# Layer 0 of a two-layer graph attention kernel: units of two heads by half of the rows, with part of the row sums on GpSimd

## The chip, the cores and the metric

The kernel runs on one NeuronCore of a Trainium2 chip. The metric is the device time of one launch in microseconds; lower is better. A core has five engines that run side by side and meet through semaphores: TensorE (PE; its weight loads are shown apart as PEld), VectorE (DVE), ScalarE (ACT), GpSimd (POOL) and SyncE (SP), which here issues most of the DMAs. Each engine works through its own queue in order, so an instruction that waits holds up what is behind it. The working memory SBUF has 128 partitions; PSUM, where TensorE writes its results, has eight banks of 512 f32 per partition.

## The reference

Two attention layers over a graph of N = 2048 nodes, 8 batches, D = 256 features. All values are f32. Shortened:

```python
# layer 0: 8 heads of 32 features; beta = softplus(beta_tilde), adj doubles as the prior
e    = leaky_relu(e_src[:, None] + e_dst[None, :], 0.2) + beta * log(adj + 1e-6)
attn = softmax(where(adj > 0, e, -inf), axis=-1)
h    = attn @ (x @ W[head])                     # per head, then joined
x1   = layernorm(x + h @ W_out.T)
# layer 1: one head
e    = leaky_relu((x1 @ W1) @ (x1 @ W2).T, 0.2)
out  = layernorm(x1 + relu(softmax(where(adj > 0, e, -1e12)) @ (x1 @ W3)))
```

## The kernel before, in words

**Layer 0.** The exponential of a leaky ReLU of a sum is the larger of two products. After common factors are divided out, a weight of head h, key j and query i is `max(c[i], r[j]) * m[j, i] * e[j]`, where c belongs to the query, r and e to the key (both lie in the tile `re`), and m is the masked prior, the same for all heads and batches. The keys lie on the partitions, so 2048 keys are 16 key tiles `jt`, and the queries ("rows" of the attention matrix) lie along the free dimension.

A batch has four head pairs `hp` of two heads. A *step* (`Gat.step`, L355) is one head pair and one key tile. In it VectorE makes `s = max(c, r) * m` for each of the two heads over all 2048 rows (L391), one 128x2048 tile per head; `c` is a row of 2048 numbers copied to all partitions by a DMA (`query_rows`, L325), and `mt` is the transposed prior of this key tile, made once by `make_m` and `make_mt` in batch 0 and read again from DRAM by `load_mt` (L206) for every head pair of every batch. TensorE multiplies s by the values (`products`, L421): `val` collects s times v, where v has been multiplied by e beforehand (`scale`, L303), and `den` collects the row sums, s times e. Each of these matmuls is 32 columns of weights wide and 512 rows long; four of them, two heads by two stretches of rows, stand beside each other on the four 32-partition strips of the array.

For the row sums there is a second way. For the key tiles listed in `SUMMED` (L68), VectorE adds `s * e` into a tile `d` per head (L404; the first of them is written by ScalarE, L409), and TensorE sums `d` once at the end, with weights of one. `SUMMED` is empty for the first head pair of each batch and for batch 0; it has six key tiles in the other head pairs of batch 1 and eight of batches 2 to 7.

When a head pair is done, `finish` (L428) copies val and den out of PSUM on ScalarE, sends den through SBUF and DRAM to be inverted and spread over partitions, and VectorE multiplies. It is a generator; each later step advances it by one stage.

**Layer 1.** The class `Dot` works on the batch before, one query tile of 128 rows per `Dot.step` (L575): TensorE makes scores `e` in four chunks of 512 (L564), between them transposes the last tile's exponentials (`pt`, L590), ScalarE evicts both (`p`, L566, and `pts`, L592), VectorE masks and finds the maximum (L569), ScalarE takes the exponential (L572), and TensorE multiplies by the values into `acc` (L607), which ScalarE evicts into `z` (L612). Between two batches come `output` (layer 0's last product y, L493, and its normalization) and `turn` (the transposes and products that layer 1 starts from).

**The order.** TensorE's order is that of the program text throughout, and from the end of batch 0 on SP's is too (L93, L693). The loop at the end interleaves the layers: it gives each part of layer 1 a number of layer-0 steps to issue after its `acc` (the list at L735, together 64 steps per batch). The order on VectorE, ScalarE and GpSimd is set by the compiler's scheduler, which goes by what is ready and by the order of the text. Batch 0 of layer 0 runs alone, beside the projections of the other batches.

**Buffers.** s tiles come from a ring of eight tiles of 8 KB per partition (tag "s"), which also holds layer 1's p and for some time a tile of heads (`ht`). `mt` has two buffers, c two, and "d" two, which in places also serve as further mt buffers. PSUM: val and den two banks each, acc one, and three banks that all other products share in turn (`mm_tile`, L80).

Of the kernel before, what the change touches and what calls it, by code (L numbers as in the profile page):

```python
# [27 lines left out]
def kernel(  # L28
# [39 lines left out]
    SUMMED = [[()] * NP, [()] + [(0, 3, 6, 8, 11, 14)] * (NP - 1)]  # L68
    SUMMED += [[()] + [tuple(range(0, NT, 2))] * (NP - 1)] * (B - 2)

# [12 lines left out]
    def ring_tile(name, shape=(P, N)):  # L83


        return wide.tile(list(shape), F32, tag="s", name=name, bufs=8)
# [75 lines left out]
    mt_d = dram.tile([N, N], F32, name="mt_d")  # L162
# [4 lines left out]
    rec_d = dram.tile([B, NP // 2, 2, 2, HP, HALF], F32, name="rec_d")  # L167
# [16 lines left out]
    def make_m(jt):  # L184

        a = wide.tile([P, NT, P], I32, tag="d", name="adj_t", bufs=2)
        nc.sync.dma_start(a, adj[:, ts(jt, P)].rearrange("(t p) j -> p t j", p=P))
        m = ring_tile("m", (P, NT, P))
        nc.vector.tensor_scalar(m, a, 0.0, None, ALU.max)
        nc.scalar.activation(m, m, AF.Ln, bias=eps_prior)  # L190
        nc.scalar.activation(m, m, AF.Exp, scale=beta_c)
        nc.vector.scalar_tensor_tensor(m, a, 0.0, m, ALU.is_gt, ALU.mult)
        return m

    def make_mt(jt, m):

        mt = wide_tile("mt", "mt", 2)
        for g in range(NB):
            t = mm_tile("mtp")
            for k in range(IG):  # L200
                nc.tensor.transpose(t[:, ts(k, P)], m[:, g * IG + k, :], ident)
            nc.scalar.copy(mt[:, ts(g, BK)], t)
        nc.sync.dma_start(mt_d[ts(jt, P), :], mt)
        return mt

    def load_mt(jt, tag="mt"):  # L206
        mt = wide_tile("mt", tag, 2)
        nc.sync.dma_start(mt, mt_d[ts(jt, P), :])
# [40 lines left out]
    class Gat:  # L249


        def __init__(self, b):
            self.b = b
            self.units = ((hp, jt) for hp in range(NP) for jt in range(NT))
# [48 lines left out]
        def scale(self, hp):  # L303

            v = self.v[hp].rearrange("p t (a f) -> p t a f", a=HP)
            e = self.re[:, 1, :, ts(hp, HP)]
            nc.vector.tensor_tensor(v, v, e.unsqueeze(3).to_broadcast([P, NT, HP, DH]), ALU.mult)
# [17 lines left out]
        def query_rows(self, h):  # L325

            c = wide_tile("c", "c", 2)
            nc.sync.dma_start(c, c_d[self.b, h:h + 1, :].to_broadcast([P, N]))
            return c

        def load_ahead(self):

            self.mt_loads = (load_mt(jt, "d" if hp == 0 and jt in (4, 5, 8, 9) else "mt")
                             for b in range(self.b, B) for hp in range(NP) for jt in range(NT))
            self.c_loads = (gats[b].query_rows(h) for b in range(self.b, B) for h in range(H))
            self.mts, self.cs_ahead = [], []
            for _ in range(HP):
                self.cs_ahead.append(next(self.c_loads))  # L340
                self.mts.append(next(self.mt_loads))

        def follow(self, gat):

            self.mt_loads, self.c_loads, self.mts, self.cs_ahead = gat.mt_loads, gat.c_loads, gat.mts, gat.cs_ahead
# [9 lines left out]
        def step(self, count=1):  # L355

            for _ in range(count):
                evict()
                hp, jt = next(self.units)
# [3 lines left out]
                if hp == NP - 1 and jt == 0 and self.b + 1 < B:  # L363
# [3 lines left out]
                if at < B * NP:  # L367
                    gat = gats[at // NP]
                    if jt == 4 and gat.b > 0:
                        gat.load(at % NP)  # L370
                    elif jt == 12:
                        gat.scale(at % NP)
                if jt == 0:
                    if self.b > 0:
                        self.cs = [self.cs_ahead.pop(0) for _ in range(HP)]
                    else:
                        self.cs = [self.query_rows(hp * HP + a) for a in range(HP)]
                    self.val = pacc.tile([P, HALF], F32, tag="val", name="val")
# [389 lines left out]
```

## Time and profile before

| what | value |
|---|---|
| median of 3 runs | 4270.26 us (4266.07 to 4271.94) |
| span of the profiled execution | 4267.8 us; the median of the runs is 2.5 us above it |
| TensorE busy | 4169.3 us (98%) |
| VectorE busy | 3617.9 us (85%) |
| ScalarE busy | 1606.5 us (38%) |
| GpSimd busy | 10.3 us (0%) |
| DMA | 843.52 MB, 198 GB/s on average |
| s, L391 | 1024 operations, mean 2341 ns |
| additions to d, L404 | 282 operations, mean 2342 ns |
| val and den matmuls, L424 | 8192 and 5600 records, and 336 for the sums of d |

The profile is one execution of the program. Busy time is the union of an engine's instructions; matmuls overlap in their pipeline and their ends are modelled, so a busy TensorE is not at its peak rate. A matmul of f32 is recorded as two instructions, a transpose as one. Idle time of an engine is put down to what released it last. The span falls into three parts: batch 0 of layer 0 up to about 545 us, seven stretches of 494 us in which layer 0 of one batch runs beside layer 1 of the one before, and layer 1 of the last batch alone from about 3960 us.

### The profile page before, as it was taken

How to read it: one execution, taken by the hardware profiler on the slowest of the kernel's cores; microseconds unless marked ns; L12 is line 12 of the kernel's file. 1: busy time of each engine (PE TensorE's matmuls, PEld its weight loads, DVE VectorE, ACT ScalarE, POOL GpSimd, SP SyncE). 2: the span in 40 equal slices, each digit the busy share in tenths (PEclk: the TensorE clock that was granted, in tenths of full speed). 3: DMA queues.
4: the chain of work that ended last, by engine and by line, in shares of the span. 5: the costliest groups of instructions: out<-in, count | busy, mean ns of one | idle time of the engine just before them, and what ended most of it. 6: DMA issues, size and time to landing. Idle time of an engine off the chain costs nothing.

```text
span 4267.8 us, 59104 instructions
## 1 busy us (share of the span) xinstructions
PE 4169.3 (98%) x24928; PEld 2234.3 (52%) x24928; DVE 3617.9 (85%) x2432; ACT 1606.5 (38%) x3007; POOL 10.3 (0%) x14
## 2 busy tenths in 40 slices
PE   7999999999999999999999999999999999999999
PEld 4444355555555555555555555555455555555766
DVE  6888779998899979999799988999799997998222
ACT  6522133332333333332433333333333323343554
POOL 0000000000000000000000000000000000000000
PEclk9999999999999999999999999999999999999999
DMA  7988756656455565556555474555555565553211
GB/s 240 312 281 322 243 205 225 235 203 238 175 203 201 192 212 181 193 191 226 187 203 194 161 250 166 204 194 204 204 186 189 182 233 180 203 187 136 78 48 40
DMA packets 268458, 843.52 MB, mean 198 GB/s; under 512 B 33184, under 2 KB 166304, under 8 KB 194464
## 3 DMA queue, kind: packets, MB, share of 16 engines
q1 hardware_dynamic: 232352, 806.17, 53.7%
q10 hardware_dynamic: 35840, 33.57, 2.3%
q8 instruction: 195, 3.19, 0.3%
q14 instruction: 71, 0.58, 0.0%
HBM read 763.76 MB, written 75.37 MB: 197 GB/s over the span
## 4 chain that ended last, share of the span: by engine, by line
PE 57%; DVE 26%; issue 8%; DMA 4%; ACT 4%; SPq 0%; DVEq 0%; POOL 0%; ACTq 0%; POOLq 0%
DVE s L391 16%; PE acc L607 13%; PE e L564 12%; PE val L424 12%; PE den L424 8%; DVE d L404 5%; PE pt L590 3%; DMA mt<-mt_d 2%; PE h3p L532 2%; PE proj L283 2%; PE h1p L553 2%; DVE p L569 2%; PE y L493 1%; ACT d L409 1%; DMA adj_r<-in_adj_dram 1%
## 5 line engine op out<-in xcount | busy, mean ns | idle before, releaser
L391 DVE SCALAR_TENSOR_TENSOR s<-c,re,mt 128x2048 f32<-128x2048 f32 x1024 | 2358.4, 2341 | 180.9 <-DMA mt<-mt_d 58.0
L424 PE MATMUL val<-s,v 128*32 128x512 f32 x8192 | 980.3, 598 | 24.1 <-DVE s L391 24.1
L564 PE MATMUL e<-x1t,h 128*128 128x512 f32 x2048 | 964.7, 595 | 6.1 <-ACT pts L592 5.1
L607 PE MATMUL acc<-h,pts 128*128 128x256 f32 x4096 | 907.5, 380 | 0.0
L607 PEld LDWEIGHTS acc<-h,pts 128*128 128x128 f32 x4096 | 779.5, 190 | 157.4 <-issue 57.4
L424 PE MATMUL den<-s,re 128*32 128x512 f32 x5600 | 686.2, 594 | 0.0
L404 DVE SCALAR_TENSOR_TENSOR d<-s,re,d 128x2048 f32<-128x2048 f32 x282 | 654.2, 2342 | 0.0
L424 PEld LDWEIGHTS val<-s,v 128*32 128x32 f32 x8192 | 252.6, 110 | 601.5 <-issue 528.5
L569 DVE CUSTOM_DVE_ANT_0 p<-p,pen 128x2048 f32<-128x2048 f32 x128 | 292.6, 2286 | 256.2 <-ACT p L566 256.1
L564 PEld LDWEIGHTS e<-x1t,h 128*128 128x128 f32 x2048 | 351.2, 190 | 271.7 <-issue 249.8
L566 ACT ACTIVATE p<-e 128x512 f32<-128x512 f32 x512 | 306.1, 598 | 392.9 <-PE e L564 387.5
L572 ACT ACTIVATE p<-p,neg 128x2048 f32<-128x2048 f32 x128 | 256.5, 2004 | 496.8 <-DVE neg L569 496.8
L424 PEld LDWEIGHTS den<-s,re 128*32 128x32 f32 x5600 | 190.3, 110 | 419.4 <-issue 419.0
L590 PEld LDWEIGHTS pt<-ident,p 128*128 128x128 f32 x2048 | 245.5, 141 | 301.1 <-issue 235.8
L592 ACT COPY pts<-pt 128x512 f32<-128x512 f32 x512 | 297.5, 586 | 200.3 <-PE pt L590 193.9
L590 PE MATMUL pt<-ident,p 128*128 128x128 f32 x2048 | 310.2, 276 | 15.7 <-ACT p L572 8.3
L230 ACT ACTIVATE f<-mv,eps_ln 128x1 f32<-128x1 f32 x128 | 37.9, 296 | 432.7 <-DVE mv L228 431.7
L612 ACT ACTIVATE z<-acc,rec 128x256 f32<-128x256 f32 x128 | 60.1, 470 | 288.5 <-issue 127.5
L283 PE MATMUL proj<-wp,xt 128*128 128x272 f32 (+1 forms) x512 | 130.6, 400 | 3.6 <-ACT xt L182 1.8
L532 PE MATMUL h3p<-w3s,x1t 128*128 128x256 f32 x512 | 122.7, 383 | 6.4 <-ACT x1t L527 4.7
L493 PE MATMUL y<-wot,ht 128*128 128x256 f32 x512 | 119.0, 385 | 3.5 <-ACT x1t L527 2.1
L285 ACT COPY v<-proj 128x256 f32<-128x256 f32 x128 | 47.2, 374 | 198.0 <-PE proj L283 153.5
(88 smaller groups left out, 1896.4 us busy)
## 6 DMA issues: line engine op xcount, KB each, us to landing
mt<-mt_d SPq DMA_DIRECT2D x496, 1024.0 KB
c<-c_d SPq DMA_DIRECT2D x64, 1024.0 KB
pen<-pen_d SPq DMA_DIRECT2D x112, 512.0 KB
xg<-in_x_dram SPq DMA_DIRECT2D x60, 512.0 KB
adj_t<-in_adj_dram SPq DMA_DIRECT2D x16, 1024.0 KB
mt_d<-mt SPq DMA_DIRECT2D x16, 1024.0 KB
rb<-rec_d SPq DMA_DIRECT2D x128, 128.0 KB
x_d<-ht ACTq DMA_DIRECT2D x64, 256.0 KB
```

The costliest lines, as they stand in the source:

```text
L283: nc.tensor.matmul(t[:, 0:cols], xt[kc][:, ts(it % IG, P)], wp[:, kc, 0:cols], start=(kc == 0), stop=(kc == KC - 1))
L391: nc.vector.scalar_tensor_tensor(sa, self.cs[a], self.re[:, 0, jt, h:h + 1], mt, ALU.max, ALU.mult)
L404: nc.vector.scalar_tensor_tensor(d, sa, e[:, jt - 1, h:h + 1], d, ALU.mult, ALU.add)
L424: nc.tensor.matmul(dst[ts(q, DH), ts(c, BK)], weights[q % 2], s[q % 2][:, ds(q // 2 * HALF + c * BK, BK)], start=start, stop=stop)
L532: nc.tensor.matmul(t[:, ts(i, D)], x1t[:, kc, ts(2 * (j - lag) + i, P)], w3s[:, kc, :], start=(kc == 0), stop=(kc == KC - 1))
L564: nc.tensor.matmul(t, self.h1[:, kc, ts(it % IG, P)], self.x1t[:, kc, ts(c, BK)], start=(kc == 0), stop=(kc == KC - 1))
L566: nc.scalar.activation(p[:, ts(c, BK)], t, AF.Prelu, alpha=ALPHA)
L569: nc.vector.tensor_tensor_reduce(p, p, pen, -1.0, FMAX, ALU.add, ALU.min, neg)
L572: nc.scalar.activation(p, p, AF.Exp, bias=neg, scale=-1.0, accum_out=den)
L590: nc.tensor.transpose(t[:, ts(k, P)], p[:, ts(g * IG + k, P)], ident)
L592: nc.scalar.copy(pt, t)
L607: nc.tensor.matmul(acc, pts[g][:, ts(k, P)], self.h3[:, j, :], start=(j == 0), stop=(j == NT - 1))
```

## The change

A unit of layer 0 is now two heads by *half* of the rows. A step takes two key tiles of one unit, so that there are still 64 steps per batch and 16 per head pair, and each s tile now holds both heads of one key tile over 1024 rows: it has the same size, but is written by two operations of 1024 elements. The steps run over the first half of the rows (`rh`), then over the second; the transposed prior is stored in that order, two key tiles by half of the rows to a tile.

- **c in PSUM.** c of a unit is staged in SBUF by a DMA and copied by ScalarE into two PSUM tiles of two banks each when the unit begins; VectorE reads it from there. To make room, val shrinks to one bank, den and acc become tiles of the three shared banks.
- **Row sums.** The first 10 key tiles (batch 0, except its first head pair, which has none) or 11 (all others) of each unit are multiplied by e in place, by ScalarE, before they are used. GpSimd adds these tiles into a tile `sums`. TensorE takes these tiles for val with v as it is (`scale` now leaves out their part of v), and sums the remaining 5 or 6 key tiles, and `sums`, into den.
- **Buffers.** The ring of s has nine tiles, c in SBUF one, mt two at all times.
- **The rest** follows: `finish` works on half of the rows, the first half of the first head pair's val waits in a small tile until `ht` is free, and the numbers of steps per layer-1 part are 4, 4, 4, 3, 3, 2, 4, 4, 3, 3, 2, 4, 4 instead of 4, 4, 4, 3, 3, 3, 3, 4, 3, 3, 3, 3, 4.

The diff, cut to its core:

```diff
-    SUMMED = [[()] * NP, [()] + [(0, 3, 6, 8, 11, 14)] * (NP - 1)]
-    SUMMED += [[()] + [tuple(range(0, NT, 2))] * (NP - 1)] * (B - 2)
+    J2 = NT // 2
+    SUMMED = [[0] + [10] * (NP - 1)] + [[11] * NP] * (B - 1)
...
-        return wide.tile(list(shape), F32, tag="s", name=name, bufs=8)
+        return wide.tile(list(shape), F32, tag="s", name=name, bufs=9)
...
-    mt_d = dram.tile([N, N], F32, name="mt_d")
+    mt_d = dram.tile([2 * J2, P, 2, HALF], F32, name="mt_d")
...
-    def make_m(jt):
-        a = wide.tile([P, NT, P], I32, tag="d", name="adj_t", bufs=2)
-        nc.sync.dma_start(a, adj[:, ts(jt, P)].rearrange("(t p) j -> p t j", p=P))
+    def make_m(n):
+        rh, j2 = divmod(n, J2)
+        a = wide.tile([P, NT // 2, 2 * P], I32, tag="d", name="adj_t", bufs=2)
+        nc.sync.dma_start(a, adj[ts(rh, HALF), ts(j2, 2 * P)].rearrange("(t p) j -> p t j", p=P))
...
+    def mt_tile():
+        return wide.tile([P, 2, HALF], F32, tag="mt", name="mt", bufs=2)
...
         def scale(self, hp):
-            v = self.v[hp].rearrange("p t (a f) -> p t a f", a=HP)
-            e = self.re[:, 1, :, ts(hp, HP)]
-            nc.vector.tensor_tensor(v, v, e.unsqueeze(3).to_broadcast([P, NT, HP, DH]), ALU.mult)
+            at = SUMMED[self.b][hp]
+            v = self.v[hp].rearrange("p t (a f) -> p t a f", a=HP)[:, at:]
+            e = self.re[:, 1, at:, ts(hp, HP)]
+            nc.vector.tensor_tensor(v, v, e.unsqueeze(3).to_broadcast([P, NT - at, HP, DH]), ALU.mult)
...
-        def query_rows(self, h):
-            c = wide_tile("c", "c", 2)
-            nc.sync.dma_start(c, c_d[self.b, h:h + 1, :].to_broadcast([P, N]))
-            return c
+        def stage(self, unit):
+            hp, rh = divmod(unit, 2)
+            self.staged = wide.tile([P, HP, HALF], F32, tag="c", name="c_in", bufs=1)
+            nc.sync.dma_start(self.staged, c_d[self.b, ts(hp, HP), ts(rh, HALF)].unsqueeze(0).to_broadcast([P, HP, HALF]))
...
-            self.mt_loads = (load_mt(jt, "d" if hp == 0 and jt in (4, 5, 8, 9) else "mt")
-                             for b in range(self.b, B) for hp in range(NP) for jt in range(NT))
+            self.mt_loads = (load_mt(n) for b in range(self.b, B) for hp in range(NP) for n in range(NT))
+            self.mts = [next(self.mt_loads) for _ in range(2)]
...
+                chain = SUMMED[self.b][hp]
+                if j2 == 0:
+                    self.c = [pacc.tile([P, HALF], F32, tag=f"c{a}", name="c") for a in range(HP)]
+                    for a in range(HP):
+                        nc.scalar.copy(self.c[a], self.staged[:, a])
+                    self.val = pacc.tile([P, BK], F32, tag="val", name="val")
+                    self.den, self.held = None, []
+                    if chain:
+                        self.sums = wide.tile([P, HP, HALF], F32, tag="d", name="sums", bufs=2)
+                elif j2 == 2:
+                    unit = self.b * NP * 2 + hp * 2 + rh + 1
+                    if unit < B * NP * 2:
+                        gats[unit // (NP * 2)].stage(unit % (NP * 2))
...
+                for i in range(2):
+                    jt = 2 * j2 + i
+                    s = ring_tile("s", (P, HP, HALF))
+                    for a, h in enumerate(heads):
+                        nc.vector.scalar_tensor_tensor(s[:, a], self.c[a], r[:, jt, h:h + 1], mt[:, i],
+                                                       ALU.max, ALU.mult)
+                    made.append((jt, s))
...
-                if jt - 1 in chain[1:]:
-                    for d, sa, h in zip(self.sums, self.last, heads):
-                        nc.vector.scalar_tensor_tensor(d, sa, e[:, jt - 1, h:h + 1], d, ALU.mult, ALU.add)
...
+                for jt, s in made:
+                    if jt < chain:
+                        for a, h in enumerate(heads):
+                            nc.scalar.activation(s[:, a], s[:, a], AF.Copy, scale=e[:, jt, h:h + 1])
+                        if jt > 0:
+                            nc.gpsimd.tensor_tensor(self.sums, made[0][1] if jt == 1 else self.sums, s, ALU.add)
+                for jt, s in made:
+                    self.products(self.val, [v[:, jt, ts(a, DH)] for a in range(HP)], s, jt == 0, jt == NT - 1)
+                    if jt >= chain:
+                        self.held.append((jt, s))
+                if j2 == J2 - 1 or NT - chain > 4:
+                    for jt, s in self.held:
+                        if self.den is None:
+                            self.den = mm_tile("den")
+                        self.products(self.den, [e[:, jt, h:h + 1].to_broadcast([P, DH]) for h in heads], s,
+                                      jt == chain, not chain and jt == NT - 1)
+                    self.held = []
+                if j2 == J2 - 1:
+                    if chain:
+                        self.products(self.den, [ones] * HP, self.sums, False, True)
+                    dn = chunk.tile([P, BK], F32, tag="ht", name="dn", bufs=4)
+                    nc.scalar.copy(dn, self.den)
+                    evictions.append((self, self.finish(hp, rh, self.val, dn)))
...
         def products(self, dst, weights, s, start, stop):
-            for c in range(HALF // BK):
-                for q in range(4):
-                    nc.tensor.matmul(dst[ts(q, DH), ts(c, BK)], weights[q % 2],
-                                     s[q % 2][:, ds(q // 2 * HALF + c * BK, BK)],
-                                     start=start, stop=stop)
+            for q in range(4):
+                nc.tensor.matmul(dst[ts(q, DH), :], weights[q % 2], s[:, q % 2, ts(q // 2, BK)], start=start, stop=stop)
...
-            acc = pacc.tile([P, D], F32, tag="acc", name="acc")
+            acc = mm_tile("acc")[:, 0:D]
...
-        for n in (4, 4, 4, 3, 3, 3, 3, 4, 3, 3, 3, 3, 4):
+        for n in (4, 4, 4, 3, 3, 2, 4, 4, 3, 3, 2, 4, 4):
```

## The prediction

> **What bounds the kernel now.** I read the page's busy times first, then the windows of the repeating stretch, then the waits and the groups inside one stretch, then the timeline of one step. One stretch, two periods long (columns: stretch, length, then busy time and count for TensorE, its weight loads, VectorE, ScalarE and GpSimd, then clock, DMA share, GB/s):
>
> ```profile
> 2187.00:2681.00 494.00, 488.68 (x2930) 257.33 (x2929) 455.88 (x299) 178.51 (x322) 0.00 (x0) 1.00 0.56 197
> 2681.00:3175.00 494.00, 488.68 (x2931) 257.56 (x2930) 456.08 (x301) 178.29 (x323) 0.00 (x0) 1.00 0.55 197
> ```
>
> The kernel repeats every 494 us: layer 0 of one batch beside layer 1 of the batch before. TensorE is busy 489 of it, VectorE 456, ScalarE 178, GpSimd 0. The groups and the waits of the first of these periods:
>
> ```profile
> L391 DVE SCALAR_TENSOR_TENSOR s<-c,re,mt 128x2048 f32<-128x2048 f32 x129 | 297.2, 2339 | 18.4 <-DMA c<-c_d 7.5 <-PE den L424 6.1 <-DMA mt<-mt_d 4.5
> L424 PE MATMUL val<-s,v 128*32 128x512 f32 x1024 | 119.6, 594 | 0.9 <-DVE s L391 0.9
> L404 DVE SCALAR_TENSOR_TENSOR d<-s,re,d 128x2048 f32<-128x2048 f32 x42 | 97.4, 2341 | 0.0
> L424 PE MATMUL den<-s,re 128*32 128x512 f32 x640 | 76.9, 592 | 0.0
> L569 DVE CUSTOM_DVE_ANT_0 p<-p,pen 128x2048 f32<-128x2048 f32 x16 | 36.5, 2283 | 14.5 <-ACT p L566 14.5
> L409 ACT ACTIVATE d<-s,re 128x2048 f32<-128x2048 f32 x6 | 12.1, 2010 | 1.8 <-DVE s L391 1.8
> ...
> PEld val L424 <- DVE s L391: 3.7, 7, 1.8
> ```
>
> TensorE waits 3.7 us for s, VectorE 6.1 us for a ring slot: VectorE is close behind, yet the matmul order sets the period. Its price per unit of work is in the timeline, where four weight loads come every 0.43 us, and score chunks every 2.15 us:
>
> ```profile
> 2761.07 0.13 PEld L424 LDWEIGHTS val<-s,v 128*32 128x32 f32 x4 [0.30 <-issue]
> 2761.49 0.13 PEld L424 LDWEIGHTS val<-s,v 128*32 128x32 f32 x4 [0.30 <-issue]
> ...
> 2772.89 1.88 PE L564 MATMUL e<-x1t,h 128*128 128x512 f32 x4
> ...
> 2774.80 0.60 ACT L566 ACTIVATE p<-e 128x512 f32<-128x512 f32 x1 [1.08 <-PE e L564]
> 2775.04 1.02 PE L564 MATMUL e<-x1t,h 128*128 128x512 f32 x2
> ```
>
> Call four matmuls of 512 columns, one per 32-row strip, a quad. It is eight recorded instructions (f32 counts twice), so 0.86 us. Check: a period has 128 val quads and 86 den quads (688 records by the den view), 214 x 0.86 = 184 us. A layer-1 step is 4 x 2.15 + 32 x 0.2135 (acc) = 15.5 us, 16 of them 248; h1 is 32 x 0.43 = 14; y, turning and h3 31 (64 + 64 records at 0.2135, 32 transposes at 0.11). Sum 477, so 17 us of 494 are latency.
>
> **What the Trainium skill says.** GPSIMD Engine Reference, § 3.1 Elementwise, gives 4497 ns for an f32 tensor_tensor add of 2048 elements; no row of this trace has a two-input GpSimd instruction. SBUF — State Buffer, § Who interferes with whom: a VectorE instruction with one SBUF input leaves GpSimd alone, one with two contends with a GpSimd read; untested in this trace, GpSimd being idle. ScalarE: Activation LUTs, § What ACT_TABLE_LOAD costs, gives 186 ns + 0.833 per element, 93 more for a pointer operand; 2048 elements make 1985, the trace has 2010 (agrees). VectorE: DVE Perf Modes, § The TRN2 errata, gives (N+151)/0.96 ns for an f32 tensor_tensor: 691 at 512, and 682 in the trace although one input is PSUM, so I charge PSUM nothing.
>
> **Part 1, row sums.** A unit is now two heads by half of the rows, so one key tile costs one quad for val. Den quads by batch, before and after: batch 0, 128 and 32 + 3 x 2 x (6+1) = 74; batch 1, 98 and 8 x (5+1) = 48; batches 2 to 7, 86 and 48. Removed: 54 + 50 + 6 x 38 = 332 quads x 0.86 = **285 us of TensorE**, on the path. VectorE loses all 282 d additions, 97.4 us per period, and eleven sixteenths of the v scaling (4 x 1.21 to about 4 x 0.48, 3 us).
>
> **Part 2, s with c in PSUM.** Twice as many half-length operations. Three of 2048 take 6.79 us in the chain, 2.27 each, 0.13 above 2048/0.96; so half length is 1.067 + 0.13 = 1.20. A period: 256 x 1.20 = 307 for 295. If the overlap of neighbours vanished or PSUM cost 60 ns, 1.27: 18 more. VectorE: 456 - 97 - 3 + 12 = **368**. Handing c over at a unit's start (ScalarE copy, about 1.04) waits for the last s and stops VectorE about 1.5 us, 8 times: 12 us, hidden under TensorE.
>
> **Part 3, ScalarE.** A scale of 1024 is 2.01 - 0.85 = 1.16 us alone, 1.065 with the overlap: 2.13 per tile. A period: 178 - 12 (L409) - 12 (old evictions, 8.1 + 4.1) + 15 (8 x (2 x 0.58 + 0.59) and the held first half) + 17 (16 c copies) + 88 x 2.13 = 187: **about 373**, double. Each scale stands between VectorE's s and both val and the addition, and behind it in ScalarE's queue wait pts, p and z, for which TensorE waits.
>
> **Part 4, GpSimd.** 10 additions a unit, 80 a period x 4.5 = **360**. Bounds: 3.5, below what the skill shows, and 6.5; I take 4.5 since no long input of VectorE but p, z, rb and v shares the port. Those 16 x (2.29 + 0.42) + 8 x 1.2 = 53 us can be waited for on either side: GpSimd 413, or VectorE about 368 + 40 x 1.8 (half an addition, at 0.8 busy) = 440. A unit of two full steps lasts 2 x 15.5 + 22 x 0.86 + 1.7 = 51.6 us on TensorE, its additions 45.
>
> **Part 5, PSUM slots.** acc and den move into the three mm slots. acc alone costs nothing: it starts after a pt slot is free, z empties it in 0.47. In units split 3, 3, 2, den stays open through one score phase, leaving two slots: p of one chunk ends at 2775.40, the next e would start at 2775.04, so 0.4 x 4 = 1.6 us, twice a period. In units split 2, 2, 2 den is open beside y's two tiles or the turning, about 2.4 us, twice. **8 us per period.** Units split 4, 4 open and close den between score phases.
>
> **Part 6, the rest.** c is staged at j2 = 2 instead of the last key tile, same 64 loads of 1 MB, SP issues them behind the previous mt load and its wait is over by then: 0. mt keeps 496 loads but only two buffers always; with 4.8 us of s per tile and loads of 5 to 8.5 us in the chain, a tile can come every 4.9 to 6.7 us, and a step takes 7: hidden, paying only above 9 us. rc loads and reciprocals go from 32 to 64 short ones; rec_d stays 64, rb 128; SP and VectorE cover them. adj loads get 1 KB rows instead of 512 B: zero, at best 10 us at the start.
>
> **Sum.** A period: TensorE 477 - 32.7 = 444, + 17 latency + 8 slots = 469. ScalarE is locally overfull: a full first step has 8 chain tiles, 17 + 9 (layer 1) + 4 (c, val, dn) = 30 us, against TensorE's 15.5 + 8 x 0.86 = 22.4; the second has 16 against 27.5. The nine ring slots (p and often ht hold two) let it work ahead, not fully: I charge 2 us in three such units, 6. So 475, 19 less. In all: 285 - 7 x 14 - 21 (the start, 60 to 545 us, waits for mt and s too; I count on 25 of its 46) = 166. Span 4267.8 - 166 = 4102; the runs' median stands 2.5 above the span, so **4104 us**.
>
> **Rivals.** (B) Everything hides and TensorE's whole saving arrives: 4270 - 285 = 3985, to 4040 with part of the slots. For it: TensorE waits only microseconds today beside a VectorE at 92%. Against: four engines at 80% or more. (C) GpSimd becomes the bound: at 5.6 us an addition plus 3 us between units, 8 x 59 = 472, hardly above my period, but at 5.8 it is 488: 6 x 7 + 25 = 67 saved, 4203. (E, the other side) ScalarE's queue: a pts or p copy stands behind a scale that waits for a tile not yet made. My whole gain is 166/(7 x 16) = 1.5 us per layer-1 step; above that the change loses. At one scale (1.1) and one s operation (1.2) per step it is 2.3 x 112 = 258: 4360. For it: today's slack of e's slots is about 1.3 us, a little over one scale, and ScalarE doubles. Against: the tiles of the first step can be scaled in the light second one. (S) The gain is lost exactly: 4262 to 4279.
>
> **How the numbers follow.** My case (4040 to 4180) 0.42, B 0.12, C (4180 to 4261) 0.10, S 0.04, E 0.32. Within 0.2% is no change that this measurement can tell. Faster 0.64, same 0.04, slower 0.32. The range, 4000 to 4340, leaves out the best of B (0.03) and the worse half of E (0.15).
>
> **What would show it.** Den matmuls fall from 5600 + 336 records to about 3280; s reads about 1.2 to 1.27 us x 2048; GpSimd has 614 additions, 4.5 us from start to start; ScalarE's share is near 70%; the period is near 475. I am wrong if e or pt waits long for pts or p behind scales (E), if val waits for the scaled s, if additions are 5.8 us apart without a gap (C), or if p's VectorE operation takes several microseconds more beside an addition.

## The result, and the profile after

| | before | after |
|---|---|---|
| median | 4266.11 us (4264.96 to 4271.94) | 4825.64 us (4802.89 to 4836.06) |
| span of the profiled execution | 4267.8 us | 4801.1 us |
| TensorE granted clock, mean | 0.995 | 0.946 |

The medians are of five runs each. The change makes the kernel slower: the ratio is 1.13, 95% interval 1.1275 to 1.1326, against a forecast of 4104 us. Of the four runs of the experiment e14 below, two were in a slower state of the chip (4905 and 4916 us), and its time is the mean of the other two (4812 and 4828). The busy times of the page of after:

```profile
PE 4211.4 (88%) x22272; PEld 2210.6 (46%) x22272; DVE 3692.2 (77%) x3206; ACT 3059.5 (64%) x4548; POOL 2990.0 (62%) x628
```

TensorE fell from 98% to 88% of its span, and no engine took its place at the top. The windows of two stretches of after, in the columns that the prediction explained (the first holds 256 operations on s and 16 on p, which is the work of one period):

```profile
1551.00:2100.00 549.00, 487.33 (x2625) 254.75 (x2624) 452.58 (x388) 365.34 (x522) 391.22 (x81) 0.95 0.52 177
2100.00:2650.00 550.00, 486.84 (x2617) 254.79 (x2616) 449.21 (x388) 363.73 (x519) 389.88 (x81) 0.94 0.51 176
```

A period lasts about 550 us where it lasted 494, and each of the four engines is idle for 60 us of it or more. The groups of after by line (before had L404 and L409 for row sums, and 2283 ns for the p of one step):

```profile
L410 POOL TENSOR_TENSOR sums<-sums,s 128x2048 f32<-128x2048 f32 x552 | 2696.0, 4884 | 174.2 <-ACT s L408 112.0 <-issue 21.4
L399 DVE SCALAR_TENSOR_TENSOR s<-c,re,mt 128x1024 f32<-128x1024 f32 x2048 | 2493.5, 1271 | 242.6 <-DMA mt<-mt_d 173.1 <-POOL sums L410 26.1 <-ACT c L376 11.5
L408 ACT ACTIVATE s<-s,re 128x1024 f32<-128x1024 f32 x1352 | 1513.7, 1153 | 263.8 <-DVE s L399 258.6 <-ACT z L238 0.9
L572 PE MATMUL e<-x1t,h 128*128 128x512 f32 x2048 | 1054.3, 641 | 153.6 <-ACT pts L600 96.6 <-ACT h L563 31.1 <-ACT p L574 25.9
L577 DVE CUSTOM_DVE_ANT_0 p<-p,pen 128x2048 f32<-128x2048 f32 x128 | 515.2, 4025 | 483.9 <-ACT p L574 483.7
L433 PE MATMUL den<-s,re 128*32 128x512 f32 x2784 | 365.1, 597 | 0.0
L621 DVE TENSOR_TENSOR z<-z,x1r 128x256 f32<-128x256 f32 x128 | 210.6, 1646 | 99.8 <-ACT z L620 98.5 <-DMA rb<-rec_d 1.2
L475 DVE TENSOR_TENSOR ht<-ht,rb 128x1024 f32<-128x1024 f32 x32 | 120.2, 3756 | 6.2 <-DMA rb<-rec_d 6.2
```

TensorE's den work fell as counted. VectorE's operations on s cost 1271 ns, the upper price. But VectorE's operations with two inputs in SBUF grew: p from 2286 to 4025 ns, z (L621) from 420 to 1646, ht (L475) from 1215 to 3756. The last two in before:

```profile
L613 DVE TENSOR_TENSOR z<-z,x1r 128x256 f32<-128x256 f32 x128 | 53.8, 420 | 61.6 <-ACT z L612 61.6
...
L467 DVE TENSOR_TENSOR ht<-ht,rb 128x1024 f32<-128x1024 f32 x32 | 38.9, 1215 | 5.6 <-DMA rb<-rec_d 5.6
```

The waits of after (engine, tile and line, what it waited for: us in all, times, longest):

```profile
ACT p L580 <- DVE neg L577: 418.1, 128, 11.6
PEld val L433 <- ACT s L408: 293.5, 226, 14.1
ACT s L408 <- DVE s L399: 258.6, 151, 6.8
...
DVE s L399 <- DMA mt<-mt_d: 173.1, 111, 9.2
...
PE e L572 <- ACT pts L600: 96.6, 38, 4.4
```

The waits form a chain: TensorE waits for scaled s and for pts, both come from ScalarE, ScalarE waits for VectorE's s and for p's minimum (`neg`). Why VectorE's minimum takes so long is in the timeline of after, VectorE's lines first, then GpSimd's, then ScalarE's (start and length in us):

```profile
2623.27 6.38 DVE L577 CUSTOM_DVE_ANT_0 p<-p,pen 128x2048 f32<-128x2048 f32 x1 [4.05 <-ACT p L574]
...
2634.29 4.73 DVE L621 TENSOR_TENSOR z<-z,x1r 128x256 f32<-128x256 f32 x1
...
2622.95 4.54 POOL L410 TENSOR_TENSOR sums<-sums,s 128x2048 f32<-128x2048 f32 x1
...
2627.57 6.55 POOL L410 TENSOR_TENSOR sums<-sums,s 128x2048 f32<-128x2048 f32 x1
...
2634.19 4.55 POOL L410 TENSOR_TENSOR sums<-sums,s 128x2048 f32<-128x2048 f32 x1
...
2629.69 2.00 ACT L580 ACTIVATE p<-p,neg 128x2048 f32<-128x2048 f32 x1 [3.34 <-DVE neg L577]
...
2640.25 1.15 ACT L408 ACTIVATE s<-s,re 128x1024 f32<-128x1024 f32 x1 [3.95 <-DVE s L399]
```

An addition ends at 2622.95 + 4.54 = 2627.49. The p operation, begun at 2623.27, ends at 2629.65, which is 2.16 us later: it stood still through nearly the whole addition and then ran at its usual speed. Now the next addition stands still in its turn, 6.55 us for 4.54. The z operation, 0.42 us of work, begins 0.10 us after an addition, at 2634.29, and ends 0.28 us after that addition does (2638.74). ScalarE stands idle for 3.34 and 3.95 us behind the two. Taking each of the 128 p operations of this trace in this way (start plus length, against the ends of all additions): 89 are more than 0.1 us over their 2.28 us, and each of these ends 2.15 us, within 0.015, after the end of an addition.

### The profile page after: what moved, and what is told of

Its sections match the earlier page's. It is cut to its first block, busy times and chain, and to the rows that moved or that the text cites. A ratio compares the mean times of both kernels' runs of the same rounds, so it can differ in the third digit from the quotient of the medians.

```text
span 4801.1 us, 57717 instructions
## 1 busy us (share of the span) xinstructions
PE 4211.4 (88%) x22272; PEld 2210.6 (46%) x22272; DVE 3692.2 (77%) x3206; ACT 3059.5 (64%) x4548; POOL 2990.0 (62%) x628
## 4 chain that ended last, share of the span: by engine, by line
DVE 29%; PE 28%; ACT 13%; issue 10%; DMA 7%; POOL 2%; SPq 0%; DVEq 0%; ACTq 0%; POOLq 0%
DVE s L399 15%; PE e L572 11%; PE acc L615 8%; DMA mt<-mt_d 6%; ACT s L408 6%; DVE p L577 6%; DVE z L621 3%; PE val L433 3%; PE pt L598 2%; POOL sums L410 2%; PE den L433 2%; ACT p L574 2%; PE h3p L540 1%; ACT p L580 1%; DVE pen L224 1%
## 5 line engine op out<-in xcount | busy, mean ns | idle before, releaser
L410 POOL TENSOR_TENSOR sums<-sums,s 128x2048 f32<-128x2048 f32 x552 | 2696.0, 4884 | 174.2 <-ACT s L408 112.0
L399 DVE SCALAR_TENSOR_TENSOR s<-c,re,mt 128x1024 f32<-128x1024 f32 x2048 | 2493.5, 1271 | 242.6 <-DMA mt<-mt_d 173.1
L408 ACT ACTIVATE s<-s,re 128x1024 f32<-128x1024 f32 x1352 | 1513.7, 1153 | 263.8 <-DVE s L399 258.6
L433 PE MATMUL val<-s,v 128*32 128x512 f32 x8192 | 1133.2, 617 | 156.2 <-ACT s L408 105.5
L410 POOL TENSOR_TENSOR sums<-s 128x2048 f32<-128x2048 f32 x62 | 290.2, 4681 | 1113.6 <-ACT s L408 1113.6
L577 DVE CUSTOM_DVE_ANT_0 p<-p,pen 128x2048 f32<-128x2048 f32 x128 | 515.2, 4025 | 483.9 <-ACT p L574 483.7
L433 PE MATMUL den<-s,re 128*32 128x512 f32 x2784 | 365.1, 597 | 0.0
L621 DVE TENSOR_TENSOR z<-z,x1r 128x256 f32<-128x256 f32 x128 | 210.6, 1646 | 99.8 <-ACT z L620 98.5
L376 ACT COPY c<-c_in 128x1024 f32<-128x1024 f32 x128 | 130.3, 1018 | 140.4 <-DVE s L399 129.4
L433 PEld LDWEIGHTS den<-s,re 128*32 128x32 f32 x2784 | 97.1, 111 | 212.3 <-issue 200.7
```

The costliest lines, as they stand in the source:

```text
L399: nc.vector.scalar_tensor_tensor(s[:, a], self.c[a], r[:, jt, h:h + 1], mt[:, i], ALU.max, ALU.mult)
L408: nc.scalar.activation(s[:, a], s[:, a], AF.Copy, scale=e[:, jt, h:h + 1])
L410: nc.gpsimd.tensor_tensor(self.sums, made[0][1] if jt == 1 else self.sums, s, ALU.add)
L433: nc.tensor.matmul(dst[ts(q, DH), :], weights[q % 2], s[:, q % 2, ts(q // 2, BK)], start=start, stop=stop)
L577: nc.vector.tensor_tensor_reduce(p, p, pen, -1.0, FMAX, ALU.add, ALU.min, neg)
L621: nc.vector.tensor_add(z, z, xr)
```

## The experiments

The layer-0 product y is made once per batch, so its first matmul ends the start and its last one the repeating part; what follows the last y is 287 us in every trace. I call the time to the first y the *start*, and from the first to the last the *repeat*, seven periods. They come from the view of the tile y of each profile. Of e14 only the times are used. Each ratio is to the runs of before that were made beside the run.

| run | median us | ratio to before (95%) | start | repeat |
|---|---|---|---|---|
| before | 4266.11 | 1 | 497.5 | 3483.7 |
| after | 4825.64 | 1.13 (1.1275 to 1.1326) | 600.3 | 3914.0 |
| e1_one_add | 4257.07 | 0.9977 (0.997 to 0.9985) | 548.3 | 3416.0 |
| e2_no_scale | 4604.04 | 1.0785 (1.0768 to 1.0802) | 594.0 | 3722.4 |
| e3_neither | 4174.44 | 0.9777 (0.9762 to 0.9793) | 544.1 | 3333.2 |
| e10_neither_mt3 | 4098.66 | 0.9607 (0.9592 to 0.9621) | 507.9 | 3300.5 |
| e12_after_mt3 | 4761.4 | 1.1164 (1.1146 to 1.1183) | 606.4 | 3867.8 |
| e7_one_input | 4640.97 | 1.0882 (1.0863 to 1.0901) | 602.1 | 3741.6 |
| e8_clean_ports | 4422.94 | 1.0361 (1.0338 to 1.0383) | 600.4 | 3517.1 |
| e11_self_add | 4583.75 | 1.0741 (1.0725 to 1.0757) | 587.7 | 3707.8 |
| e13_split | 5004.78 | 1.1758 (1.17 to 1.1816) | 622.3 | 4093.0 |
| e14_split_mt3_b0 | 4820.0 (two runs) | 1.1298 (1.1272 to 1.1323) | | |
| e15_six | 4691.08 | 1.1007 (1.0987 to 1.1027) | 521.7 | 3849.5 |
| e4_b0_plain | 4743.9 | 1.1124 (1.1092 to 1.1156) | 551.0 | 3906.3 |
| e9_no_allreduce | 4787.09 | 1.1218 (1.1199 to 1.1237) | 570.8 | 3934.4 |
| e5_after_all_pe | 4641.13 | 1.0883 (1.0867 to 1.0899) | 540.3 | 3813.2 |
| e6_before_all_pe | 4458.5 | 1.0453 (1.0437 to 1.0469) | 493.7 | 3675.8 |

Two theories stood at the beginning. P: VectorE's operations with two inputs in SBUF and GpSimd's additions cannot read at the same time, since they share a port into SBUF, and what follows on VectorE waits too. A: ScalarE's queue of scales holds up what stands behind it, the prediction's rival E.

### Additions, scales, both

e1 leaves out all GpSimd additions but the first of each unit, e2 the multiplications on ScalarE, e3 both:

```diff
-                        if jt > 0:                                     # e1, e3
+                        if jt == 1:
-                        for a, h in enumerate(heads):                  # e2, e3
-                            nc.scalar.activation(s[:, a], s[:, a], AF.Copy, scale=e[:, jt, h:h + 1])
```

> The changed kernel with only the first GpSimd addition of each unit left (62 of 614); the row sums lack nine or ten key tiles, so the output is not the reference's. ScalarE's scales, the PSUM slots and TensorE's work stay. Theory P (VectorE's operations with two SBUF inputs wait for GpSimd's additions, and everything behind them on VectorE): p returns from 4.0 to about 2.3 us, z's addition from 1.65 to 0.42, VectorE's busy time falls by about 590 us, and the kernel falls from 4826 to between 4000 and 4250. Theory A (ScalarE's queue: scales in front of pts, p and z): the time stays above 4600. Theory S (half rows, PSUM slots): above 4600 too.

> The changed kernel with ScalarE's 1352 scales left out (the weights of these key tiles lack the factor e, so the output is not the reference's); all 614 additions stay. Theory P: p still takes about 4 us and the kernel stays above 4600, at most 200 below 4826. Theory A: below 4300.

> Both left out, the scales and all but the first addition of a unit (output not the reference's). This is what TensorE's shorter work would give if all else were hidden. Theory S (half rows with c in PSUM and den and acc in the shared PSUM slots cost time themselves): above 4150. My prediction's sum (332 quads less, 8 us per period for slots): 3985 to 4060.

Additions cost 569 us beside the scales (4825.64 - 4257.07) and 430 without them (4604.04 - 4174.44). Scales cost 83 us without additions and 222 beside them. e1 ends 7 us above the range of theory P, and e2 falls by 222 us where P allowed 200, while theory A missed both by hundreds. Both costs are real, the additions are by far the larger, and each makes the other dearer by 139 us; why is not shown. Without additions p is fast again, while TensorE still waits for scaled s. The groups by line, then the waits, of e1:

```profile
L577 DVE CUSTOM_DVE_ANT_0 p<-p,pen 128x2048 f32<-128x2048 f32 x128 | 296.6, 2317 | 470.5 <-ACT p L574 470.5
...
L621 DVE TENSOR_TENSOR z<-z,x1r 128x256 f32<-128x256 f32 x128 | 53.7, 419 | 117.1 <-ACT z L620 115.0 <-DMA adj_r<-in_adj_dram 2.2
...
PEld val L433 <- ACT s L408: 253.9, 216, 9.7
```

With neither, 4174 is still 70 us above the forecast. The next pair of runs looks for the cause.

### Two or three mt buffers

e10 is e3, and e12 is after, with three mt buffers, loads three tiles ahead, and a ring of eight s tiles to pay for the room:

```diff
-        return wide.tile([P, 2, HALF], F32, tag="mt", name="mt", bufs=2)
+        return wide.tile([P, 2, HALF], F32, tag="mt", name="mt", bufs=3)
-                    while len(self.mts) < 2 and (mt := next(self.mt_loads, None)):
+                    while len(self.mts) < 3 and (mt := next(self.mt_loads, None)):
```

> e3 (no scales, one addition a unit; output not the reference's) with three mt buffers instead of two and eight ring tiles instead of nine, so that the third mt takes the room of a ring tile. In e3 VectorE waited 215 us for mt and TensorE some 300 for s. If the two mt buffers cost what separates e3 (4174) from my sum (3985): 4000 to 4100. If the ring or the slots do: 4150 or more.

> The changed kernel whole (output is the reference's) with three mt buffers and eight ring tiles. By its 173 us of VectorE's waits for mt: if they are on the path, 4700 to 4780; if they only fill time that VectorE would spend waiting for something else, 4800 to 4850; if the ring tile is missed more, above 4850.

The third buffer is worth 76 us without the row-sum work and 64 with it. VectorE's waits for mt in e3, and then in e10:

```profile
DVE s L399 <- DMA mt<-mt_d: 214.7, 153, 5.9
```

```profile
DVE s L399 <- DMA mt<-mt_d: 30.9, 14, 5.9
```

e10 does what the prediction's sum supposed, with nothing on ScalarE and GpSimd in the way, and comes to 4099 us. That this is within 6 us of the forecast is luck: its start is 35 us worse than forecast, and it does not pay the 42 us that the forecast charged for ScalarE. The repeat is the better comparison. It is 183 us below before; the forecast's own share for this, without ScalarE's 6 us per period, was 285 - 46 (the start) = 239 of TensorE less 7 x 8 for PSUM slots, 183 as well. It is no kernel to use, since it leaves out the scales and all additions but one per unit.

### Which of VectorE's operations wait, and for what

e7 replaces p's masked minimum of two inputs by a minimum of one, leaving out the mask. e8 also leaves out the scaling of v and the multiplication of ht, and adds z straight from PSUM, so that it has one input in SBUF (without the ReLU):

```diff
-            nc.vector.tensor_tensor_reduce(p, p, pen, -1.0, FMAX, ALU.add, ALU.min, neg)     # e7, e8
+            nc.vector.tensor_reduce(neg, p, AX.X, ALU.min)
-            nc.vector.tensor_add(z, z, xr)                                                    # e8
+            nc.vector.scalar_tensor_tensor(z, acc, rec, xr, ALU.mult, ALU.add)
-            nc.vector.tensor_mul(half, half, rb)                                              # e8
```

> The changed kernel with layer 1's masked minimum replaced by a plain minimum of p, so that VectorE's longest operation of layer 1 has one SBUF input instead of two (the mask is left out, the output is not the reference's). Everything else stays, all 614 additions too. Theory P, the port: that operation takes about 2.3 us instead of 4.0, VectorE does 220 us less, the wait of the exponential for it falls by half, and the kernel falls by 100 to 300 us. If the additions hurt by anything else (ring slots held, ScalarE order), it stays within 50 of 4826.

> The changed kernel with the same 614 additions and all scales, but no VectorE operation with two SBUF inputs left in the repeating stretch, save one of four elements: p's minimum without the mask, z's addition reading acc from PSUM (without the ReLU), the multiplications of heads by the inverted row sums and of v by e left out (output not the reference's). Theory P whole: what the additions cost, 569 us by e1, is the port, and this kernel is within 60 us of e1, 4200 to 4320. If ring slots held by GpSimd and its late sums matter as much as the port: 4400 to 4560.

The groups of e8:

```profile
L410 POOL TENSOR_TENSOR sums<-sums,s 128x2048 f32<-128x2048 f32 x552 | 2523.7, 4572 | 166.4 <-ACT s L408 102.9 <-issue 22.3
...
L576 DVE TENSOR_REDUCE neg<-p 128x1 f32<-128x2048 f32 x128 | 292.1, 2282 | 496.2 <-ACT p L573 496.2
L620 DVE SCALAR_TENSOR_TENSOR z<-acc,rec,x1r 128x256 f32<-128x256 f32 x128 | 61.5, 480 | 124.0 <-ACT z L619 123.8
```

GpSimd does the same additions on the same data beside it, and p takes 2282 ns, z 480. In the repeat, where the additions had cost 498 us (3914.0 - 3416.0), e7 recovers 172 and e8 397. Some 55 of the 397 are plain work that e8 leaves out (32 multiplications of ht at 1.2 us, 32 scalings of v at about 0.5), so about 340 of the 498 go with the waits of these four operations. e8's repeat is still 101 above that of e1, and its 4423 us lie not where theory P alone put them (up to 4320) but in the range for a further cause (4400 to 4560). Two operations still run long in it: f, four elements with two inputs, at 1698 ns on average (154 in before), and the making of pen from adjacency rows at 1912 (687 in before). Over 32 operations of each this is some 89 us of VectorE more than in before. The additions also hold s tiles; how the 101 us divide is not shown. The case of pen is not the theory's: it has one input, and converts integers to bf16.

e11 asked about those tiles: from the second on, an addition adds `sums` to itself and does not read s.

```diff
-        nc.gpsimd.tensor_tensor(self.sums, made[0][1] if jt == 1 else self.sums, s, ALU.add)
+        nc.gpsimd.tensor_tensor(self.sums, made[0][1] if jt == 1 else self.sums, s if jt == 1 else self.sums, ALU.add)
```

> The changed kernel with the same number of additions of the same length, but from the third key tile of a unit on GpSimd adds sums to itself, so that s tiles are no longer held for it (row sums wrong, output not the reference's). Theory P: the port is as busy as before, the time stays at 4720 to 4830. If ring slots held for GpSimd are the cause: below 4500.

It is 242 us faster than after, between the two ranges, and settles nothing, since such an addition is also shorter (3875 ns). The groups of e11:

```profile
L410 POOL TENSOR_TENSOR sums<-sums 128x2048 f32<-128x2048 f32 x552 | 2138.8, 3875 | 57.0 <-issue 13.9
L577 DVE CUSTOM_DVE_ANT_0 p<-p,pen 128x2048 f32<-128x2048 f32 x128 | 394.7, 3083 | 474.0 <-ACT p L574 474.0
```

That s tiles are held by GpSimd shows as 26.1 us of waiting in after (the group of L399 above); how much it costs beyond that stays open.

### How long a wait is: whole additions or pieces

If a wait lasts for one GpSimd instruction, shorter instructions should help. e13 writes each addition as four of 512 columns; e14 adds the third mt buffer and leaves batch 0 to TensorE; e15 is e14 with six additions per unit in place of ten:

```diff
-                            nc.gpsimd.tensor_tensor(self.sums, made[0][1] if jt == 1 else self.sums, s, ALU.add)
+                            was = made[0][1] if jt == 1 else self.sums
+                            for a in range(HP):
+                                for i in range(2):
+                                    nc.gpsimd.tensor_tensor(self.sums[:, a, ts(i, BK)], was[:, a, ts(i, BK)],
+                                                            s[:, a, ts(i, BK)], ALU.add)
-    SUMMED = [[0] + [10] * (NP - 1)] + [[11] * NP] * (B - 1)
+    SUMMED = [[0] * NP] + [[11] * NP] * (B - 1)      # e14; e15 has 7 in place of 11
```

> The changed kernel with each GpSimd addition of 2048 columns written as four of 512; the same sum is computed. Theory 1, a two-input operation of VectorE waits until the GpSimd instruction in progress ends, so that its wait is as long as that one instruction: pieces of about 1.2 us (a quarter of the 4564 ns of the whole) cut the masked minimum of p from 4.0 us to 2.7-3.0, the z addition from 1.65 to about 0.8, and the kernel to 4550-4720. Theory 2, it waits until GpSimd has no more work back to back: the minimum of p stays at 3.8-4.2 us and the kernel at 4800 or above, up to 4900 by the fixed cost of four instructions for one.

> As the run with the additions in four pieces, with three mt buffers and a ring of eight s tiles, and without the additions of the first batch; the same output. The two repairs were worth 64 us (three buffers) and 82 us (first batch) alone, so about 146 us below the run with pieces alone if they add up: 4400-4580 if pieces work, about 4660-4750 if they do not. To beat the kernel before (4266) the pieces would have to take away nearly all of the waits of VectorE.

> As the run before it, with six additions per unit instead of ten, so 80 quads of row sums per period on TensorE where there were 48: 27 us of TensorE per period more, some 190 in all, against two fifths less of GpSimd's time on the port and so two fifths less of the waits left. If the waits are what remains: 4350-4550. If pieces have already removed the waits, this is slower than the run before it by 100-200 us.

Pieces make it slower, 5005 us, and neither theory of the expectation holds alone. The view of the tile p of e13 (durations min/median/max in ns), and its timeline, VectorE and then GpSimd:

```profile
L581 DVE CUSTOM_DVE_ANT_0 p<-p,pen x128: 2276/2793/19144, 739.4 to 4981.1; 128x2048 f32<-128x2048 f32 x128
```

```profile
2140.63 2.98 DVE L581 CUSTOM_DVE_ANT_0 p<-p,pen 128x2048 f32<-128x2048 f32 x1
...
2176.62 15.07 DVE L581 CUSTOM_DVE_ANT_0 p<-p,pen 128x2048 f32<-128x2048 f32 x1 [0.78 <-ACT p L578]
...
2110.75 49.10 POOL L413 TENSOR_TENSOR sums<-sums,s 128x512 f32<-128x512 f32 x36
...
2174.76 14.78 POOL L413 TENSOR_TENSOR sums<-sums,s 128x512 f32<-128x512 f32 x12
```

The median p fell to 2793 ns, as for a wait of one piece: the one at 2140.63 got through in 2.98 us amid an unbroken run of additions. The one at 2176.62 waited to the end of a run, 2174.76 + 14.78 = 2189.54, and ended 2.15 us after it. In the whole trace 77 p operations waited more than 0.1 us, and each ended 2.15 us, within 0.02, after the end of a piece. 37 of them got in while the run of pieces went on, after at most 1.15 us. The other 40 waited for a pause of GpSimd, and these make 447 of the 473 us of waiting in all. With whole additions no p of after waited longer than 4.4 us: it got its turn at the next addition's end. A difference that the trace shows: whole additions stand 0.08 us apart (2622.95 + 4.54 to 2627.57 above), while twelve pieces take 14.78 us, 1.23 each, though one piece alone lasts 1.28 in the median, so a piece begins before its predecessor has ended. That this keeps VectorE out is argued, not shown, and why it got in 37 times stays open.

The two repairs in e14 bring 185 us where 146 were expected, by two runs only, and six additions per unit instead of ten bring 129 more, although row sums go back to TensorE. Both times lie outside all the ranges given for them. So fewer additions serve better, and still 4691 is 425 us above before. No version that computes the whole result with the additions came nearer.

### The start, and PSUM

e4 leaves the additions and scales of batch 0 out and sums there on TensorE (`SUMMED = [[0] * NP] + [[11] * NP] * (B - 1)`). e9 replaces the reduction over partitions that makes the factors of each batch, on GpSimd, by a copy of one half of `top` on VectorE, which leaves the maximum out:

```diff
-            nc.gpsimd.partition_all_reduce(top[:, 1, :], top[:, 0, :], P, bass_isa.ReduceOp.max)
+            nc.vector.tensor_copy(top[:, 1, :], top[:, 0, :])
```

> The changed kernel with no key tiles for GpSimd in batch 0 (its row sums all on TensorE; the output is the reference's). It adds 54 quads, 46 us of TensorE work, to the start. Theory Q (batch 0 is lost to GpSimd's own queue: the partition reductions of the other batches' factors stand behind additions, with about 11 us of idle time around each, and TensorE waits in order for what they release): the start shortens from about 680 to about 560 us and the kernel falls by 80 to 130 us, to 4700 to 4745. Theory P alone (the start is lost to ports only): a fall of 20 to 60 us. If TensorE's extra work counts: no fall or a rise.

> The changed kernel with GpSimd's eight reductions over partitions replaced by a copy on VectorE (each partition keeps its own maximum; output not the reference's). Additions stay in batch 0. Theory Q: GpSimd's queue and the idle time of about 11 us around each reduction are gone; the start shortens by about 60 to 90 us and the kernel by as much, to 4735 to 4765, about what e4 gained in spite of 46 us more of TensorE work. If batch 0 is lost to ports and scales instead: less than 30.

Without any GpSimd additions in batch 0 the start is 49 us shorter, although TensorE has 128 - 74 = 54 quads, 46 us, more to do. Without the reductions it is 30 us shorter, less than theory Q's 60 to 90. The medians fall by 82 and 39 us; part of that is that the profiled execution of after was the fastest of its five. GpSimd's timeline of after around one reduction:

```profile
578.76 0.39 POOL L298 PARTITION_ALL_REDUCE top<-top  x1 [11.16 <-issue]
585.88 14.63 POOL L410 TENSOR_TENSOR sums<-sums,s 128x2048 f32<-128x2048 f32 x3 [6.72 <-issue]
```

An instruction of 0.39 us costs GpSimd 18 us among additions: the trace has instructions that change GpSimd's configuration (MODIFY_POOL_CONFIG) on both sides of it. The Trainium skill, GPSIMD Engine Reference, § 2.1 Instruction dispatch, gives about 6 us for loading a kernel's code at its first call. The last six reductions of after stand among additions; GpSimd was idle for 5.9 to 11.2 us before them and 6.7 to 13.1 after, so the shortest pauses agree, though these are not first calls.

e5 and e6 put all row sums on TensorE, in the changed structure (`[[0] * NP] * B`) and in the kernel before (`[[()] * NP] * B`), so that only the structure differs.

> The changed kernel with no key tile on GpSimd or ScalarE: all row sums on TensorE, as e6 has them in the old units, with the same 2048 quads. The difference between the two is what the new units, c in PSUM, the shared PSUM slots and the two mt buffers cost or bring by themselves. From e3 (4174, while my sum without losses gave 3985): if the structure costs some 100 us or more, e5 is at least 60 above e6. If it is free, they agree within 20. By TensorE's work (1306 quads more than none, 82 a period above the old 86 + 128) both lie near 4500 to 4620.

> The old kernel with all row sums on TensorE (no additions to d). 1024 den quads instead of 742, 282 more at 0.86 = 243 us on TensorE, VectorE 654 us less: 4266 + 243 = 4510 if TensorE sets the time, between 4450 and 4520.

The structure, with its two mt buffers, costs 183 us when den is open all the time: 47 in the start, 137 in the repeat. e5's expectation put both near 4500 to 4620; e5 came out above it (4641) and e6 below (4458). With den holding one of three PSUM slots the score chunks come slower; e5's timeline of the matmuls of e, from one chunk's start to the next:

```profile
2507.28 1.99 PE L572 MATMUL e<-x1t,h 128*128 128x512 f32 x4 [0.25 <-ACT p L574]
...
2509.95 1.98 PE L572 MATMUL e<-x1t,h 128*128 128x512 f32 x4 [0.25 <-ACT p L574]
```

2.67 us per chunk, where three slots gave 2.15.

## Why the prediction was wrong, point by point

The loss can be put together from the table, each line being the difference of two runs:

| what, and the runs | start | repeat | in the forecast |
|---|---|---|---|
| structure and fewer row sums on TensorE: e10 - before | +10 | -183 | -25 and -183 |
| two mt buffers: e3 - e10 | +36 | +33 | 0 |
| scales on ScalarE: e1 - e3 | +4 | +83 | 6 per period, 42 |
| additions on GpSimd: after - e1 | +52 | +498 | 0 |
| sum: after - before | +103 | +430 | -25 and -141 |

103 + 430 = 533 is the difference of the two spans; that of the medians is 560, since the profiled execution of after was 25 us below its median. e9's repeat, whose work is that of after, is 20 us longer, so shares that contain after are good to some 20 us. The shares hold in this order: taken off first, the scales would be worth 222.

- **Part 1, row sums: right.** 2784 records for s and 496 for `sums` make the 3280 foretold. e10 shows that their time comes back where nothing else stands in the way.
- **Part 2, s with c in PSUM: the size was at its upper bound.** 1271 ns for 1.20 us, 18 us of VectorE per period, for which e10 shows no price.
- **Part 3, ScalarE: the load was right, its price not.** 365 us per period for 373 foretold. But I charged 2 us in three units, those split 4, 4. The cost is 83 us in all where nothing else is late, which is 12 per period for 6, and it lies elsewhere: in e1, for each of batches 3 to 7, the weight loads of val wait about 12 us for scaled s in the second unit and 7 in the third, which run mostly in steps of two, beside y, the turning and the first scores, and at most 0.3 in a unit split 4, 4.
- **Part 4, GpSimd and the port: the loads were right, and the step that failed is how they entered the sum.** GpSimd 391 us per period, between 360 and 413. VectorE 451, where I had worked out 440 for the case that it does all the waiting (40 waits of 1.8 us, 72; measured in the first stretch: p 68 for 37, z 29 for 7, ht 14 for 5, v 11 for about 2, so 72 more). The sum then charged none of it: 440 lies below TensorE's 444. Loads side by side are covered; these waits are not side by side. The p operation stands between the scores and their transposes, in a TensorE order fixed by the program text, and holds up the s behind it that ScalarE scales and TensorE needs next. What was put at nothing measured 498 / 7 = 71 us per period, of which e8 and e1 leave up to 101 / 7 = 14 to other causes. That VectorE's waiting comes to about as much is no proof, since TensorE pays in two ways: in the repeat it is busy for 3459 us and idle for 455 in after, busy for 3292 and idle for 124 in e1. So 331 of the 498 us are idle time, and 167 are the same matmuls running longer, which the last section looks at. The working had the warning in its last sentence, p taking several microseconds more beside an addition, and gave it no price. Its list of VectorE operations that the additions can hold up (p, z, rb, v) also lacked f and pen.
- **Part 5, PSUM slots: right in kind, and small.** 0.52 us per chunk for 0.4; e10's repeat leaves no room for a large error.
- **Part 6: "hidden" was wrong for mt.** Loads pay above 9 us, I wrote, but with two buffers VectorE waited 173 us in after and 215 in e3; a third buffer was worth 64 and 76. It also overlooked GpSimd's own queue: the reductions that were alone on it now stand among additions, 30 us in the start.
- **The start:** -25 foretold, +103 measured: mt 36, additions 52 with the reductions in it, scales 4, and 10 even in e10, which I can't place.
- **The rivals.** E, a slower kernel by ScalarE's queue, had the right sign and a real mechanism, but the smaller one: 83 us alone. B, everything hidden, did not hold even in e10 (4099). C, GpSimd as the bound, did not happen: the median addition takes 4564 ns, in e8 the mean is 4572, and GpSimd is idle for 158 us of 549. The Trainium skill, GPSIMD Engine Reference, § 3.1 Elementwise, has 4497 for it. The rule in SBUF — State Buffer, § Who interferes with whom, that the operation which comes second waits for the whole of the first, is what the trace of after shows. e13 shows more than that: 33 of its 77 waits, of 4.9 us and more, lasted over several GpSimd instructions. I read the rule as a price on a load and not as a wait in a chain.

## What to carry to other kernels

Four engine loads that all fit do not make a period: where TensorE's order is fixed and work passes through VectorE and ScalarE within a step, an operation that may stand still for several microseconds is charged to the path and not to the engine's idle time. Before moving elementwise work to GpSimd, list every VectorE operation with two inputs in SBUF, the tiny ones too, and ask who waits for each. A minimum with one input, or an addition with one of its operands left in PSUM, was out of it here (2282 and 480 ns in e8), but one input is no guarantee: the conversion of pen has one and went from 687 to 2164 ns. And when a change takes away a buffer, ask what waits with the number that remains: 76 of the 167 us by which e10 is below before hang on the third mt buffer.

## What the runs showed that I had not expected

- A wait can be many times the waiting operation's own length: f, a two-input operation of four elements, went from 154 to 962 ns on average, and up to 3.4 us.
- GpSimd waits too: its addition of 4.54 us took 6.55 when p had got in first.
- Quarter-length additions made the longest p operation longer, 19.1 us for 6.6, since VectorE does not always get a turn between them.
- A pause of TensorE costs more than its own length. The same 22272 TensorE instructions were busy for 4211 us in after and 3973 in e10; e's matmuls took 641 ns on average for 595, and the mean granted clock was 0.946 for 0.997. TensorE's timeline of after shows where:

```profile
1948.63 1.47 PE L572 MATMUL e<-x1t,h 128*128 128x512 f32 x2 [3.48 <-ACT h L563]
...
1953.06 1.06 PE L598 MATMUL pt<-ident,p 128*128 128x128 f32 x4
1953.91 2.98 PE L572 MATMUL e<-x1t,h 128*128 128x512 f32 x4
1956.73 0.60 PE L598 MATMUL pt<-ident,p 128*128 128x128 f32 x4
1957.16 1.88 PE L572 MATMUL e<-x1t,h 128*128 128x512 f32 x4
```

Behind the two pauses, of 3.48 us and of 1.09 us before 1951.19, four transposes take 1.06 us and four score matmuls 2.98; from 1956.73 on the same take 0.60 and 1.88. In the repeat of after 773 matmul instructions took more than 1.3 times the median of their kind. All of them begin within 6 us of the end of a pause of 1 us or more, stretches that make up 18% of the repeat, and all fall into times for which the trace has the granted clock at half: 430 us of the repeat in after, 72 in e1. Of the 90 stretches at half clock in the whole trace, 89 begin within 7 us after such a pause began. So the pause comes first and the low clock follows. No run varied the pauses alone.
